# Two levels of Strassen for layer 1's scores, with part of the key sums added by transfers and the layer norm's root moved from k to q

## The chip, the core and the metric

The kernel runs on one core of one Trainium2 chip. The time is device microseconds of one execution; the figure for a kernel is the median of its runs. All data are fp32. The engines are named as the profile names them: PE is TensorE (PEld its weight loads), DVE is VectorE, ACT is ScalarE, POOL is GpSimd, SP is SyncE, which here only issues transfers.

## The reference

The input x is a batch of 8 items, each 512 channels by 1024 tokens (32 x 32). Two attention layers follow one another. Layer 0 is a layer norm over the channels and an attention of 8 heads of 64 channels; layer 1 is a group norm over 32 groups and an attention with a single head of 512 channels. Cut to what matters (biases and the affine parts of the norms left out):

```
# layer 0, per item
xn = layer_norm(x)                          # over channels
q, k, v = xn @ Wq.T, xn @ Wk.T, xn @ Wv.T   # 8 heads of 64
x = softmax(q k.T / 8) v @ Wo.T + x
# layer 1, per item
h = group_norm(x)                           # 32 groups
q, k, v = wq h, wk h, wv h                  # 512 x 1024 each
attn = softmax(q.T k * 512 ** -0.5)         # 1024 x 1024, over the keys
x = x + wp (attn v)
```

The change touches layer 1's scores `q.T k`, the sums of their exponentials over the keys, and the norm of layer 0 of a later item.

## The kernel before

**Products.** A product of two matrices, each cut into 2 x 2 blocks, is done by one level of Strassen (Winograd's form): seven block products in place of eight, with sums of blocks ahead of them (S1 to S4 of the left matrix, T1 to T4 of the right) and sums of results after them. The class `Product` runs the seven steps in the order of `STEPS`, each into a PSUM bank called x, y or z; some steps accumulate into a bank that already holds another product, so that most of the sums after are made by PE. `multiply()` issues a step's matmuls. `leave()` issues what follows it: after steps 1, 3 and 4 a copy of a bank by ACT (`u(0, 0)`, `u(0, 1)`, `u(1, 1)`), after steps 2, 5 and 6 an add of a bank to such a copy by DVE (an "out", L388), after step 7 a last copy. A unit is a `Product` for 128 rows of each block of the result. An out must read its bank before PE can open that bank again, one or two steps later.

**Two levels.** The projections of k and q of layer 0 (`project_deep`, matmuls at L591) already run two levels: six of the seven outer block products are again done by seven inner products, in three pairs ("tandems", two products at a time, so that each has the other's step in between), and one outer product (`22` by `T4`) whole (L634). Their operands come from `deep_operands_later`: four DVE instructions for a block, one of 512 columns and two or more of 256.

**Order.** Each engine works through its own instructions in the program's order. The order is written out by hand in one long loop over the items. `later(...)` puts closures into a list `side`; `tick(n)`, called in each step of a `Product`, takes `n` of them (the unit's `pieces`); `until(...)` takes them until a condition holds. So DVE's sums are strewn between PE's steps. A class `LayerNorm` makes the mean and the root for item b + 2 ahead of time, from its own list; `ln.waiting` holds its root back until the main loop sets it to False.

**An item's layer 1**, with the stages' names and their times in item 0: `qa` (280 to 307.7 us), the query in the basis of h, from the group norm's `gn` blocks; `s`, the scores, 28 steps (307.7 to 355.8); `vm`, the values (355.8 to 380.0); `o`, the output, whose moving operand is the exponentials p with the sums T1 to T4 of their blocks (380.0 to 428.0). Then k and q of the next item's layer 0 (428 to 467), and its attention.

**The scores** are one level in four units (`scores`, L500): each of the 28 steps has two matmuls of 512 columns. Exp is taken on 512 columns at a time after the outs (L1132), or straight out of PSUM. Key sums: p is [keys, queries], and the sum over keys is needed for each query. `key_sums` adds p's blocks on DVE (L1155, L1157) to two sums of 1024 elements per partition; POOL then issues transfers that add the upper half of a sum's partitions onto the lower (`halve`, L719) and lay the rest side by side (`fold`, L715). `inverse` transposes that on DVE (`fold1t`, L723), takes reciprocals, lets ACT copy the rows eight times (`rr`, L1200) and expands them (`rden`, L709), by which every out of `o` is multiplied (L1233).

**The next layer norm** runs in between: POOL adds x's blocks into `lns` by accumulating transfers and folds them (`fold_mu`); on DVE `foldm` (L723) is turned into means, ACT copies them (`lnmur`, L796), DVE expands them to `mu` and subtracts them from x (L816), ACT squares, DVE adds (`lnq`), POOL folds again, and the root (Ln and Exp on ACT, and eight small copies) is released in k's seventh step.

**Transfers.** SP's queue loads the weights (`load_w`), stores and loads the blocks put away (`x1_away`, `v_away`), loads x for item b + 2 and stores the output. POOL's queue has the accumulating transfers: those above, and those which add `x1_away` to an output block (L1235).

The functions that the change touches:

## Time and profile before

| | before |
|---|---|
| median of three runs | 2872.74 us (2872.62 to 2872.74) |
| the profiled execution's own time | 2871.5 us |
| its span | 2869.6 us |
| granted TensorE clock | 0.999 |
| PE busy | 2844.8 us, 10199 matmuls |
| DVE, ACT, POOL busy | 1818.1, 1168.0, 448.7 us |

An fp32 matmul of the program is two instructions in the profile. A PE row's duration includes the time in its pipeline and overlaps the next; what a matmul costs on a busy PE is the distance to the next start. A time on a row counts from the span's start. The window of item 2's layer 1 (`qa` from 984.8 us, scores from 1012.3, `vm` from 1060.3, `o` from 1084.5, k from 1132.6, q from 1155.9 to 1177.8) is taken where one item stands for the others, since items 0 and 7 have edges of their own.

### The profile page before, as it was taken

The numbers are of one execution on the slowest core, as the hardware profiler recorded it, in microseconds if no ns is written. First come the engines' busy times: TensorE is split into PE (matmuls) and PEld (weight loads), VectorE is DVE, ScalarE is ACT, GpSimd is POOL, SyncE is SP. The second block draws the span as 40 slices with busy tenths as digits, with TensorE's granted clock in tenths as the row PEclk, the third lists the DMA queues.
The fourth block names the chain that finished last, engine by engine and source line by source line (L and its number), as shares of the span: only waits on it lengthen the run. The fifth ranks groups of instructions, "written<-read, shape, count | busy, mean of one in ns | idle before, by whom it ended". The sixth has DMA issues, their size and how long they took to land.

```text
span 2869.6 us, 29155 instructions
## 1 busy us (share of the span) xinstructions
PE 2844.8 (99%) x10199; PEld 1482.1 (52%) x10199; DVE 1818.1 (63%) x2428; ACT 1168.0 (41%) x2015; POOL 448.7 (16%) x625
## 2 busy tenths in 40 slices
PE   9999999999999999999999999999999999999999
PEld 4535455354553555535555455544556445563345
DVE  6667367773667646776467754768456774457734
ACT  4462324723257132561336513365223733236331
POOL 2021021210212101120012200121011210112000
PEclk9999999999999999999999999999999999999999
DMA  8135246351563525434264342734326431262212
GB/s 314 50 73 141 72 98 184 71 154 63 131 155 70 148 72 162 116 77 140 88 180 86 84 135 81 198 77 114 118 74 184 108 104 59 73 170 63 88 37 67
DMA packets 124251, 321.33 MB, mean 112 GB/s; under 512 B 17872, under 2 KB 22272, under 8 KB 124096
## 3 DMA queue, kind: packets, MB, share of 16 engines
q0 software_dynamic: 45120, 110.66, 21.0%
q1 hardware_dynamic: 78880, 208.70, 20.6%
q8 instruction: 82, 1.34, 0.2%
q14 instruction: 73, 0.60, 0.1%
q10 hardware_dynamic: 96, 0.02, 0.0%
HBM read 187.72 MB, written 62.39 MB: 87 GB/s over the span
## 4 chain that ended last, share of the span: by engine, by line
PE 98%; DVE 1%; DMA 1%; ACT 0%; issue 0%; POOL 0%; SPq 0%; DVEq 0%; POOLq 0%
PE s L994 16%; PE acc L1012 15%; PE x_s L500 8%; PE x_o L508 8%; PE x_v L492 4%; PE x_qa L483 4%; PE x_vm L492 4%; PE y_o L508 4%; PE y_s L500 4%; PE x_out L483 4%; PE y_v L492 2%; PE y_vm L492 2%; PE y_out L483 2%; PE z_o L508 2%; PE z_s L500 2%; PE y_qa L483 2%
## 5 line engine op out<-in xcount | busy, mean ns | idle before, releaser
L1003 DVE TENSOR_TENSOR sum<-sum,p 128x1024 f32<-128x1024 f32 x384 | 470.3, 1225 | 38.7 <-DVE sum L1003 0.5
L997 ACT ACTIVATE p<-s 128x1024 f32<-128x1024 f32 (+1 forms) x608 | 478.8, 984 | 15.2 <-PE s L994 15.2
L994 PE MATMUL s<-q,k 64*128 64x512 f32 x2048 | 448.1, 592 | 0.0
L1012 PE MATMUL acc<-p,v_again 128*64 128x512 f32 x1792 | 390.9, 594 | 0.0
L994 PEld LDWEIGHTS s<-q,k 64*128 64x128 f32 x2048 | 195.9, 186 | 248.0 <-issue 152.9
L1012 PEld LDWEIGHTS acc<-p,v_again 128*64 128x64 f32 x1792 | 126.1, 137 | 261.3 <-issue 236.7
L715 POOL DMA_DIRECT2D fold<-sum x312 | 209.3, 762 | 311.1 <-DMA sum<-sum 191.7
L719 POOL DMA_DIRECT2D sum<-sum x78 | 63.5, 814 | 1109.8 <-DVE sum L1157 339.2
L1001 DVE TENSOR_TENSOR sum<-p,p 128x1024 f32<-128x1024 f32 x64 | 78.1, 1220 | 149.0 <-ACT p L997 149.0
L1016 ACT COPY o<-acc 128x512 f32<-128x512 f32 x63 | 36.9, 586 | 221.6 <-PE acc L1012 221.4
L500 PE MATMUL x_s<-S_qa,T_gn 128*128 128x512 f32 x256 | 120.3, 592 | 0.0
L508 PE MATMUL x_o<-T_p,S_vm 128*128 128x512 f32 x256 | 115.2, 592 | 0.0
L388 DVE TENSOR_TENSOR p<-u(1, 1)_s,x_s 128x512 f32<-128x512 f32 x32 | 22.0, 687 | 128.8 <-PE x_s L500 122.3
L492 PE MATMUL x_vm<-w_m,T_gn 128*128 128x256 f32 x384 | 90.7, 379 | 0.0
L483 PE MATMUL x_qa<-T_gn,w_a 128*128 128x512 f32 x192 | 89.4, 594 | 0.8 <-ACT qa L526 0.8
L483 PE MATMUL x_out<-T_o,w_o 128*128 128x512 f32 x192 | 89.2, 594 | 0.0
L513 ACT COPY u(0, 0)_v<-x_v 128x512 f32<-128x512 f32 x16 | 9.4, 586 | 187.5 <-PE x_v L492 187.5
L500 PEld LDWEIGHTS x_s<-S_qa,T_gn 128*128 128x128 f32 x256 | 48.6, 190 | 61.2 <-issue 61.2
L492 PE MATMUL x_v<-w_v,T_h 128*128 128x256 f32 x336 | 80.0, 381 | 0.0
L508 PEld LDWEIGHTS x_o<-T_p,S_vm 128*128 128x128 f32 x256 | 48.6, 190 | 60.7 <-issue 60.7
L1058 ACT COPY rr<-r 32x16 f32<-32x16 f32 x256 | 53.5, 209 | 62.4 <-DVE r L961 59.0
L1132 ACT ACTIVATE p<-p 128x512 f32<-128x512 f32 x96 | 60.2, 627 | 45.5 <-DVE p L388 45.5
(464 smaller groups left out, 4744.2 us busy)
## 6 DMA issues: line engine op xcount, KB each, us to landing
sum<-sum POOLq DMA_DIRECT2D x78, 256.0 KB, 3.4
fold<-sum POOLq DMA_DIRECT2D x312, 64.0 KB, 2.4
x<-in_x_dram SPq DMA_DIRECT2D x32, 512.0 KB, 6.0
xr<-in_x_dram SPq DMA_DIRECT2D x64, 256.0 KB, 2.8
x_away<-x SPq DMA_DIRECT2D x32, 512.0 KB, 2.6
v_away<-v SPq DMA_DIRECT2D x28, 512.0 KB, 3.0
v_again<-v_away SPq DMA_DIRECT2D x28, 512.0 KB, 8.3
w_o<-saved_o SPq DMA_DIRECT2D x24, 512.0 KB, 4.8
```

Of the source, the lines that this page charges most:

```text
L483: nc.tensor.matmul(dst, a[:, k, ts(r, P)], b[:, k, :], start=(opens and k == 0), stop=(k == 1), skip_group_check=True)
L492: nc.tensor.matmul(dst[:, ts(m, CB)], b[:, k, ts(2 * r + m, P)], a[:, k, :], start=(opens and m == 0 and k == 0), stop=(k == 1), skip_grou ...
L500: nc.tensor.matmul(dst, b[:, k, ts(r, P)], a[:, k, :], start=(opens and k == 0), stop=(k == 1), skip_group_check=True)
L508: nc.tensor.matmul(dst, a[:, m, ts(r, P)], b[m // 2][:, m % 2, :], start=(opens and m == 0), stop=(m == NM // 2 - 1), skip_group_check=True)
L715: nc.gpsimd.dma_start(out=f[ts(q + i, BL), :], in_=t[ts(n, BL), ts(i, HB)], accum_op=ALU.add if n else ALU.bypass)
L719: nc.gpsimd.dma_start(out=t[:D, :], in_=t[D:, :], accum_op=ALU.add)
L994: nc.tensor.matmul(parts[i], self.k[m // 4][r, ts(m % 4, P)], self.q[r, :], start=True, stop=True)
L997: nc.scalar.activation(dst, src, AF.Exp, scale=1.0 / float(D) ** 0.5)
L1001: nc.vector.tensor_add(self.sum, self.p[0], p)
L1003: nc.vector.tensor_add(self.sum, self.sum, p)
L1012: nc.tensor.matmul(acc[i * D : (i + 1) * D, :], value_of(self.vt, m, self.c * P + i * D, D), self.p[m][:, ts(i, HB)], start=(m == 0), stop ...
L1132: nc.scalar.activation(p, s, AF.Exp, scale=float(C) ** -0.5)
```

## The change

The scores are computed by two levels of Strassen. `SINGLES` lists the six outer products that are done by an inner level; they run in three pairs as the projections of k and q do, with matmuls of 256 columns, and the product `22` by `T4` is done whole, a quarter of it in each of four steps of the first two pairs. The sums of the outer level can no longer be left to PE, since each inner product ends in SBUF: DVE adds the seven results (`adds`, `add`), and Exp is taken when a block of p is complete, on 1024 columns. The operands for the inner level are made by DVE: `deep_query` for the query, `deep_operands_later` for gn. The residual adds (ACT, with the store of `x1_away`) move from the scores to `qa`.

Of the key sums, the first add of each of the two sums stays on DVE (`key_sum`); the four others become accumulating transfers of 512 KB on POOL's queue (`more_sums`), ahead of `halve` and `fold`. T1 of p is made at the end of the scores, T2 to T4 in `vm`. The load of w_m is issued after the first pair. In `o`, `inverse` is issued after two steps of both units instead of after the first step of the first, and the layer norm's list is queued after one more round of `side`. The root of the layer norm is released in q's third step instead of k's seventh.

Its core:

```diff
+SINGLES = [("11", "11"), ("12", "21"), ("S2", "T2"), ("S3", "T3"), ("S1", "T1"), ("S4", "22")]
...
+        def deep_query(self, *names):
+            def first(n):
+                x = self.q[n]
+                t = made[n] = big_tile(f"{n}_deep_qa_{self.b}").rearrange("p (i t) -> p i t", i=4)
+                nc.vector.tensor_add(t[:, 0], x[:, 0, CB:], x[:, 1, CB:])
+                nc.vector.tensor_sub(t[:, 2], x[:, 0, :CB], x[:, 0, CB:])
+            def rest(n):
+                x, t = self.q[n], made[n]
+                nc.vector.tensor_sub(t[:, 1], t[:, 0], x[:, 0, :CB])
+                nc.vector.tensor_sub(t[:, 3], x[:, 1, :CB], t[:, 1])
...
+            def plain(g, c):
...
+                ps = wides[(2 - g) % 3][:, ts(c, HB)]
+                for k in range(2):
+                    nc.tensor.matmul(ps, self.hb["T4"][:, k, ts(2 * g + c, P)], self.q["22"][:, k, :],
+                                     start=(k == 0), stop=(k == 1), skip_group_check=True)
+                return lambda: nc.scalar.copy(whole6[g][:, c, :], ps)
...
+            for j in range(3):
+                units = [unit(2 * j + n) for n in range(2)]
+                for i in range(len(STEPS)):
+                    for u in units:
+                        u.multiply()
+                    copy = plain(j, i - 3) if j < 2 and i in (3, 4) else nothing
+                    tick(self.pieces[j])
+                    for u in units:
+                        u.leave()
+                    copy()
+                m1, m2, m3, m5, m4, m7 = made
+                if j == 0:
+                    adds(m2, m1)
+                    finish("11", m2)
+                elif j == 1:
+                    self.key_sum(0, "11")
+                    adds(m3, m1)
+                    adds(m5, m3)
+                    adds(whole6, m5)
+                    finish("12", whole6)
                 else:
+                    adds(m3, m4)
+                    adds(m7, m3)
+                    self.key_sum(1, "12")
+                    later(lambda: add(m5[0], m4[0]))
+                    finish("21", m7)
+                    later(lambda: add(m5[1], m4[1]))
+                    later(lambda: self.more_sums(0, "21"))
+                    finish("22", m5)
+                    self.operands("T1")
+                    side.insert(len(side) - 1, lambda: (self.more_sums(1, "22"), self.fold()))
+                yield
...
+        def more_sums(self, i, n):
+            for t in self.p[n]:
+                nc.gpsimd.dma_start(out=self.total[i], in_=wide(t), accum_op=ALU.add)
...
-            wm_now = load_w("m", b)
...
+            for n, (_, name) in enumerate(SINGLES):
+                deep_operands_later(h1b, h1_deep, [name])
+                later(*(lambda ik=ik: residual(*ik) for ik in away[n : n + 1]))
...
+            steps = whole.scores(h1_deep)
+            next(steps)
+            wm_now = load_w("m", b)
+            next(steps)
+            next(steps)
+            whole.operands("T2", "T3", "T4")
...
-            o_units[0].step(1)
-            whole.inverse()
...
-            o_units[0].step(1)
+            o_units[0].step(2)
+            o_units[1].step(2)
+            whole.inverse()
...
-                    if n == 6 and ln:
-                        ln.waiting = False
...
+                    if n == 2 and ln:
+                        ln.waiting = False
```

More of the change, by code (lines that the diff above doesn't have):

```diff
@@ L553, in operand_inner, with deep_operands_later @@
                      lambda: all(x in deep for x in names))
-    def deep_operands_later(h, deep):
+    def deep_operands_later(h, deep, names):
         def first(n):
@@ L568, in deep_operands_later @@
         made = {}
-        for _, names in TANDEMS:
-            for n in names:
-                later(lambda n=n: first(n), lambda n=n: rest(n))
+        for n in names:
+            later(lambda n=n: first(n), lambda n=n: rest(n))
     def project_deep(tag, w, w_deep, bias, h, h_deep, pieces):
@@ L1108, in __init__ @@
             self.b, self.hb, self.x1 = b, hb, x1
+            self.q_deep = {}
+            self.pieces = (2, 2, 1)
             self.q = {f"{i + 1}{j + 1}": qa[j, i] for i in range(2) for j in range(2)}
@@ L1112, in __init__, with query_sum @@
             self.t = [{}, {}]
-        def query_sums(self):
-            for n in SUM_NAMES:
+        def query_sum(self, *names):
+            for n in names:
                 sum_later(self.q, n, lambda n: block(f"{n}_qa_{self.b}"), wide)
-        def scores(self):
-            b = self.b
-            shared = [{}, {}]
-            def unit(r):
-                g = r // 2
-                def dest(i, k):
-                    p = self.p[f"{k + 1}{i + 1}"]
-                    if p[g] is None:
-                        p[g] = block(f"p1_{b}_{k}{i}_{g}")
-                    return p[g][:, r % 2, :]
-                def exponential(p, s):
-                    nc.scalar.activation(p, s, AF.Exp, scale=float(C) ** -0.5)
-                def after(i, k):
-                    if (i, k) != (1, 0):
-                        exponential(dest(i, k), dest(i, k))
-                def shift(u, ps, which, add=None):
-                    if which == (1, 0):
-                        exponential(u, ps)
-                    else:
-                        nc.scalar.copy(u, ps)
-                return Product(f"s1_{b}_{r}", self.q, self.hb, key_part(r), shift, dest,
-                               banks_of(f"s1_{b}_{g}", r % 2, shared[g]), after)
-            return [unit(r) for r in range(4)]
@@ L1149, in key_sums @@
-        def key_sums(self, g):
-            def add(i, j):
-                p = wide(self.p[f"{j + 1}{i + 1}"][g])
-                if (g, j) == (0, 1):
-                    self.total[i] = big_tile(f"sum1_{self.b}_{i}")
-                    nc.vector.tensor_add(self.total[i], wide(self.p[f"1{i + 1}"][g]), p)
-                else:
-                    nc.vector.tensor_add(self.total[i], self.total[i], p)
-                self.summed = g == 1 and i == 1 and j == 1
-            for i in range(NH):
-                for j in range(1 - g, 2):
-                    later(lambda i=i, j=j: add(i, j))
@@ L1164, in operands @@
-        def operands(self, g):
-            def sub(n, l, r):
+        def deep_query(self, *names):
[8 more added lines that the diff above has]
+                nc.vector.tensor_sub(t[:, 3], x[:, 1, :CB], t[:, 1])
+                self.q_deep[n] = t
+            made = {}
+            for n in names:
+                later(lambda n=n: first(n), lambda n=n: rest(n))
@@ new lines, in exponential, with scores, part, query_inner @@
+        def exponential(self, t):
+            nc.scalar.activation(wide(t), wide(t), AF.Exp, scale=float(C) ** -0.5)
+        def scores(self, h_deep):
+            b = self.b
+            made = [[None, None] for _ in SINGLES]
+            whole6 = [None, None]
+            wides = [wide_psum(f"s1_{b}_{n}") for n in range(3)]
+            def part(dst, a, x, opens):
+                for c in range(2):
+                    nc.tensor.matmul(dst[:, ts(c, CB)], x[0][:, ts(c, P)], a[0], start=(opens and c == 0), stop=True,
+                                     skip_group_check=True)
+            def query_inner(n):
+                x = self.q[n]
+                blocks = [{f"{i + 1}{k + 1}": x[:, k, ts(i, CB)] for i in range(2) for k in range(2)}]
+                return Inner(blocks, lambda: [{s: self.q_deep[n][:, i] for i, s in enumerate(SUM_NAMES)}],
+                             lambda: n in self.q_deep)
+            def unit(m):
+                j, r = divmod(m, 2)
+                def dest(i, k):
+                    if made[m][k] is None:
+                        made[m][k] = block(f"p1_{b}_{m}_{k}")
+                    return made[m][k][:, :, ts(i, CB)]
+                def banks(to):
+                    if to == "y":
+                        return bank(f"y_s1_{b}_{m}")
+                    return wides[(r - j) % 3][:, :HB] if to == "x" else wides[(2 - j) % 3][:, ts(r, HB)]
+                a, x = SINGLES[m]
+                until(lambda: a in self.q and x in self.hb)
+                u = Product(f"s1_{b}_{m}", query_inner(a), operand_inner(self.hb, h_deep, [x]), part, plain_shift, dest,
+                            banks)
+                u.view = lambda t: t.rearrange("p (c t) -> p c t", c=2)
+                return u
+            def plain(g, c):
+                if c == 0:
+                    whole6[g] = block(f"p1_{b}_6_{g}")
+                    until(lambda: "22" in self.q and "T4" in self.hb)
+                ps = wides[(2 - g) % 3][:, ts(c, HB)]
[3 more added lines that the diff above has]
+                return lambda: nc.scalar.copy(whole6[g][:, c, :], ps)
+            def add(t, x):
+                nc.vector.tensor_add(wide(t), wide(t), wide(x))
+            def adds(ts_, xs):
+                later(*(lambda g=g: add(ts_[g], xs[g]) for g in range(2)))
+            def finish(n, t):
+                def exponentials():
+                    for g in range(2):
+                        self.exponential(t[g])
+                    self.p[n] = t
+                later(exponentials)
+            for j in range(3):
[18 more added lines that the diff above has]
+                    finish("12", whole6)
+                else:
+                    adds(m3, m4)
[9 more added lines that the diff above has]
+                yield
@@ new lines, in key_sum, with add, operands, sub @@
+        def key_sum(self, i, n):
+            def add():
+                until(lambda: self.p[n][0] is not None)
+                self.total[i] = big_tile(f"sum1_{self.b}_{i}")
+                nc.vector.tensor_add(self.total[i], *(wide(t) for t in self.p[n]))
+            later(add)
+        def more_sums(self, i, n):
+            for t in self.p[n]:
+                nc.gpsimd.dma_start(out=self.total[i], in_=wide(t), accum_op=ALU.add)
+        def operands(self, *names):
+            def sub(n, g):
+                l, r = {"T1": ("12", "11"), "T2": ("22", "T1"), "T3": ("22", "12"), "T4": ("21", "T2")}[n]
@@ L1170, in sub @@
                     self.p[n] = [self.t[0][n], t]
-            for n, l, r in (("T1", "12", "11"), ("T2", "22", "T1"), ("T3", "22", "12"), ("T4", "21", "T2")):
-                later(lambda n=n, l=l, r=r: sub(n, l, r))
+            for n in names:
+                later(*(lambda n=n, g=g: sub(n, g) for g in range(2)))
         def fold(self):
@@ L1460, in fast_path @@
                 ln.sums()
+            h1_deep = {}
+            away = list(x1)
+            for n, (_, name) in enumerate(SINGLES):
+                deep_operands_later(h1b, h1_deep, [name])
+                later(*(lambda ik=ik: residual(*ik) for ik in away[n : n + 1]))
             for u in a_units:
-                u.rest()
+                u.pieces = 2
+            a_units[0].rest()
             whole = Whole(b, qa, h1b, x1_away)
-            s_units = whole.scores()
-            whole.query_sums()
-            later(*(lambda ik=ik: residual(*ik) for ik in x1))
-            for u in s_units[:2]:
-                u.step(2)
-            for u in s_units[:2]:
-                u.rest()
-            whole.key_sums(0)
-            whole.operands(0)
-            for u in s_units[2:]:
-                u.rest()
-            whole.key_sums(1)
-            later(whole.fold)
-            whole.operands(1)
+            whole.deep_query("11")
+            a_units[1].step(5)
+            whole.deep_query("12")
+            whole.query_sum("S1", "S2")
+            whole.deep_query("S2")
+            whole.query_sum("S3")
+            whole.deep_query("S3")
+            whole.query_sum("S4")
+            whole.deep_query("S1", "S4")
+            steps = whole.scores(h1_deep)
[4 more added lines that the diff above has]
+            whole.operands("T2", "T3", "T4")
             v_units, vm = project_v(f"vm{b}", wm_now, h1b)
-            for u in v_units:
+            for u, n in zip(v_units, (4, 3)):
+                u.pieces = (2, 1)[v_units.index(u)]
+                u.step(n)
+                u.pieces = (1, 2)[v_units.index(u)]
                 u.rest()
@@ L1482, in fast_path @@
             check = iter(()) if more else all_checks()
-            o_units[0].step(1)
-            whole.inverse()
+            for u in o_units:
+                u.at_once = False
             if ln:
                 ln.xt = load_x(b + 2)
-            o_units[0].step(1)
+            o_units[0].step(2)
+            o_units[1].step(2)
+            whole.inverse()
+            for u in o_units:
+                u.at_once = True
+                u.finish()
             next(check, None)
-            o_units[1].step(2)
-            next(check, None)
+            tick(2)
             if ln:
+                later(nothing, nothing)
                 ln.queue()
@@ L1498, in fast_path @@
             o_units[0].rest()
+            next(check, None)
             o_units[1].step(1)
@@ L1501, in fast_path @@
                 h_deep = {}
-                deep_operands_later(hb, h_deep)
+                deep_operands_later(hb, h_deep, [n for _, names in TANDEMS for n in names])
             if b == 0:
```

## The prediction

> **What bounds the kernel now.** I read the page's parts 1 and 4 first, then PE's waits. PE is busy for nearly the whole span, and the chain of work that ended last lies on it:

> ```profile
> PE 2844.8 (99%) x10199; PEld 1482.1 (52%) x10199; DVE 1818.1 (63%) x2428; ACT 1168.0 (41%) x2015; POOL 448.7 (16%) x625
> PE 98%; DVE 1%; DMA 1%; ACT 0%; issue 0%; POOL 0%; SPq 0%; DVEq 0%; POOLq 0%
> ...
> PE z_k L591 <- ACT u(0, 1)_k L607: 5.9, 5, 1.2
> ```

> The last line is the largest of PE's waits (total us, times, longest): all of them together are below 20 us of 2869.6. So a change pays only by taking matmul time from PE, and costs only where it makes PE wait. The windows of item 0 (query projection, scores, values vm, output o) show how much room the helpers have beside PE; busy us and instruction count for each engine:

> ```profile
> 280.00:307.70 27.70, 27.70 (x74) 13.87 (x73) 12.64 (x18) 6.46 (x10) 2.93 (x5) 1.00 0.26 76
> 307.70:355.80 48.10, 48.10 (x114) 21.30 (x113) 19.93 (x23) 20.39 (x35) 0.00 (x0) 1.00 0.20 71
> 355.80:380.00 24.20, 24.20 (x114) 21.31 (x113) 12.45 (x14) 5.22 (x9) 6.87 (x10) 1.00 0.49 121
> 380.00:428.00 48.00, 48.00 (x113) 21.23 (x112) 36.39 (x58) 11.80 (x28) 9.46 (x12) 1.00 0.42 90
> ```

> DVE is half free up to the o stage and three quarters taken in it. PE's timeline of item 2 shows the rows that price the matmuls, a scores step, then the projection of k, which already runs two-level products in pairs, then that wait:

> ```profile
> 1012.26 1.88 PE L500 MATMUL x_s<-qa,gn 128*128 128x512 f32 x4
> 1013.98 1.88 PE L500 MATMUL z_s<-qa,gn 128*128 128x512 f32 x4
> ...
> 1132.57 0.59 PE L591 MATMUL x_k<-x,w_k 128*128 128x256 f32 x2
> 1133.00 0.59 PE L591 MATMUL x_k<-T_h,w_k 128*128 128x256 f32 x2
> 1133.43 1.03 PE L591 MATMUL x_k<-x,w_k 128*128 128x256 f32 x4
> 1134.29 0.59 PE L591 MATMUL z_k<-x,w_k 128*128 128x256 f32 x2
> ...
> 1152.36 1.13 PE L591 MATMUL z_k<-T_deep_h,w_k_deep 128*128 128x256 f32 x4 [1.18 <-ACT u(0, 1)_k L607]
> ```

> Starts, not ends, give the price: one scores step is 1.717 us (four instructions, two logical fp32 matmuls of 512 columns); a pair step of two products is 1133.43-1132.57 plus 1134.29-1133.43, 1.72 us for eight instructions of 256 columns, without a gap.

> [...] halving the columns costs little. Agrees: 0.429 us for 512 columns, 0.2159 for 256. [...] no added sum is cheap. Agrees: 1.22 us for 1024 elements (spaced 1.14), 0.68 for 512, 0.42 for 256. [...] below, the adds behind rden start only once rr is there. [...]

> ```profile
> sum<-sum POOLq DMA_DIRECT2D x78, 256.0 KB, 3.4
> fold<-sum POOLq DMA_DIRECT2D x312, 64.0 KB, 2.4
> lns<-in_x_dram POOLq DMA_DIRECT2D x24, 512.0 KB, 5.6
> k<-k POOLq DMA_DIRECT2D x14, 512.0 KB, 8.8
> q<-q POOLq DMA_DIRECT2D x14, 512.0 KB, 5.9
> ```

> **The change, part by part.** T is the start of the scores, all times per item, eight items.

> *Scores on PE.* Removed: 28 steps, 28 x 1.717 = 48.07 us. Added: three pairs of seven steps, 21 x 1.727 = 36.27, and the whole product with T4, eight matmuls of 512 columns, 8 x 0.858 = 6.87. 43.14 in all: 4.93 less an item, **39.5 us** less over eight. This is on the path.

> *DVE.* Added: six more outs (18 for 12) of 0.69, 4; deep query blocks, 6 x 4 x 0.42, 10; deep operands of gn, 6 x (0.68 + 2 x 0.42), 9; fourteen combining adds of 1.22, 17. Removed: four key-sum adds, 5. Some 35 us, which lifts DVE from 63% to about 73%. Where it falls: the gn operands and "11", "12" of the query beside the qa stage (15 us free), the rest beside the pairs (28 us free), the last adds and the T operands in vm. Placed by each step's due time, the first pair's outs come about 0.6 us before PE wants their bank, those of the later pairs 1 us or more. In vm about 21 of 24 us are taken; PE's slack at its fifth and sixth steps is 0.1 to 0.2. I charge 0.25 there, **+2** in all; from 0 to 1 us an item, since no row of before has vm so full. If the cover is gone, the outs of vm's steps five and six are late.

> *ACT.* Eight residual adds of 0.66 move into qa, where ACT has 21 us free; Exp runs in 1024-element pieces of about 1.05 in place of 0.63 halves. ACT is 40% busy in the old scores stage: nothing. From below, zero.

> *SP and POOL.* w_m's load moves behind the first pair on SP: landing took 8 to 9 us and 28 us remain, nothing. x1_away is stored earlier and the x loads of item b+2 wait for the end of the scores; w_k comes 17 to 20 us into vm and is wanted 50 us later. On POOL, four 512 KB accumulations (p onto the two sums) stand ahead of the halves and folds, and the output adds from x_away stand behind them; those had 20 us of POOL idle before.

> *The key sums' end.* From vm's start V: the first accumulation is issued at about V+7. Two serial chains share the queue, so it is one, then two together, then one. With 6.4 us for the first, 8.1 for the second of two at once (as k's and q's landed) and 6.5 for the last beside w_k, V+28; halve and folds took 10.8 us in before from the second halve's issue to the last fold: **F = V+39**. With 5.2 us each it is V+35, with the 8.8 us median V+45.

> *The inverse.* It moves behind steps 2 of both o units. In before, everything was early:

> ```profile
> 1086.46 0.70 DVE L723 STREAM_TRANSPOSE fold1t<-fold 128x512 f32<-128x512 f32 x1
> 1090.70 1.25 DVE L709 STREAM_TRANSPOSE rden<-rr 128x1024 f32<-128x1024 f32 x1 [1.56 <-ACT rr L1200]
> 1099.84 0.70 DVE L723 STREAM_TRANSPOSE foldm<-fold_mu 64x512 f32<-64x512 f32 x1
> 1103.21 1.25 DVE L709 STREAM_TRANSPOSE mu<-lnmur 128x1024 f32<-128x1024 f32 x1 [1.76 <-ACT lnmur L796]
> 1109.04 0.68 DVE L388 TENSOR_TENSOR u(1, 1)_o<-u(1, 1)_o,x_o 128x512 f32<-128x512 f32 x1
> ```

> o begins at 1084.5 here, so fold1t ran at o+2 and foldm 13 us later. Now DVE reaches fold1t at about o+14.6 (V+38.8), and foldm, mu and the centring stand right behind. From the start s of fold1t, by these durations: rr copied at s+4.2, rden to s+5.4, two multiplications, foldm at s+6.6, lnmur copied s+8.3 to s+10.0, and only then ACT's copy of u(1, 1)_o, done at s+10.6. PE wants that bank at o+24.0 (its fifth step; before, 1106.71 against 1108.53). So s may be o+13.4, and o+14.6 makes PE wait 1.2 us, the out of u(1, 1)_o another 0.2; F at V+39.5 rather than V+38.8 adds 0.7. 2.1 us for the six items with a layer norm to come: **+12.6**. The two others have until o+15.7: nothing. If F is earlier DVE's order still gives 1.4; if the mean's DVE work ran earlier, 0.

> *Root of the layer norm.* In k its eight small ACT copies (1.70 us) stand ahead of the copy that PE waits for at 1152.36; in q's step 2 they fall where no copy is due. **-5.9**. The scaling of x moves into q's last third, where DVE is the tighter engine: 0 to 1 us an item, I take **+1.5** in all.

> *Edges.* b = 0 also makes the deep weights on DVE: **+2**; b = 7 has leading layer-norm parts in place of cover: **+1.5**; both from 0 to 4.

> Sum: -39.5 - 5.9 + 2 + 12.6 + 1.5 + 3.5 = **-25.8**, on the profiled execution's own 2871.5 us (span 2869.6): 2845.7. The median of the runs is 1.2 above that time: **2847 us**.

> **The rivals.**
> *All hidden* (foldm early or F early, no vm wait): -39.5 - 5.9 with 3 for the edges, 2830 us. For it: k's pairs run gapless with DVE as full. Against: the order of DVE's program puts foldm behind fold1t. Chance 0.25.
> *DVE becomes the bound* inside the pairs and vm, outs some tenths late at several steps: 1.5 to 2.5 us an item on top of the forecast, 2860 to 2866. For it: slack 0.6 in the first pair. Against: the 28 us free there. Chance 0.17.
> *The key sums land late, slower than before.* fold1t waits in DVE's queue for the folds and holds rden, mu, centring and every out of o behind it; ACT's copies follow. Each us that F passes V+38.8 costs one in six items, past V+39.9 in all eight. The gain left, 39.5 + 5.9 - 7, is 4.8 us an item: from F near V+42.5 on it is gone. With 8.8 us at each step and the folds slowed too, F = V+45 to V+48: 6 to 9 us an item, 2880 to 2895. For it: k<-k's median. Against: that row falls where DMA is 84% busy; vm and o were at 42 to 49%. Chance 0.12. That the scores would not shrink is excluded by the count of instructions.

> **How the numbers follow.** Forecast case 0.46, 2840 to 2858. The range goes from 2829 (all hidden) to 2872 (part of the late case), leaving a tenth above and little below. 0.2% is 5.7 us, about what a measurement of this kernel can tell from no change: faster is below 2867, which takes the first three cases, less a little: 0.85; within 0.05; slower 0.10.

> **What would show it.** Right: scores stage 43 to 44 us of PE without gaps; no z_k wait on u(0, 1)_k; 1 to 3 us of PE waits at o's steps five and six on u(1, 1)_o; fold1t idle before it below 1 us. Wrong: PE waits on outs p in the pairs (DVE bound), or fold1t waiting many us for a fold (late sums), or o without waits (all hidden).

## The result, and the profile after

The changed kernel takes 2879.39 us (median of 18 runs, 2875.08 to 2885.55), the kernel before 2872.50 beside it (18 runs, 2871.54 to 2874.00). The ratio is 1.0026, interval 1.0019 to 1.0033: **slower by 0.26%**, where 0.9% faster was forecast. The profiled execution took 2883.7 us (span 2881.6), 4.3 above its median; the differences by stage below are from it, so they add up to 12 us and not to 7. The runs of the changed kernel also lie further apart than those of before, 10 us against 2.5.

The page's parts 1 and 4:

```profile
PE 2821.9 (98%) x10775; PEld 1593.4 (55%) x10775; DVE 2069.1 (72%) x2892; ACT 1233.6 (43%) x2079; POOL 477.1 (17%) x657
PE 82%; DMA 9%; DVE 4%; issue 2%; ACT 1%; POOL 1%; DVEq 0%; SPq 0%; POOLq 0%
```

and PE's waits (us in total, times, longest):

```profile
PE y_o L509 <- ACT u(1, 1)_o L514: 13.0, 6, 2.2
PE x_q L591 <- DVE q L389: 9.9, 5, 3.6
PE x_q L591 <- DVE w_q_deep L232: 9.8, 1, 9.8
PE x_o L509 <- ACT u(0, 1)_o L514: 5.2, 5, 1.2
```

PE has less to do, and still the end is later: 9% of the chain that ended last now lies on transfers and 4% on DVE, where each had 1%, and these four waits, of which only the third was there before (2.2 us), make 38 us. The windows of item 0 for scores, vm and o, with the columns of the prediction:

```profile
308.19:351.31 43.12, 43.12 (x185) 34.96 (x184) 32.50 (x51) 18.48 (x30) 0.00 (x0) 1.00 0.03 11
351.31:375.97 24.66, 24.44 (x113) 21.18 (x112) 20.80 (x21) 10.39 (x14) 4.04 (x5) 1.00 0.75 200
375.97:427.83 51.86, 48.84 (x114) 21.03 (x113) 37.52 (x60) 12.05 (x28) 12.40 (x17) 1.00 0.48 101
```

The scores shrink from 48.07 to 43.12 us without a gap; vm and o grow. From PE's starts of all stages, time after less time before, us:

| stage | forecast | measured | by item |
|---|---|---|---|
| scores (8 items) | -39.5 | -39.5 | -4.94 to -4.95 each |
| vm (8) | +2 | +3.9 | 0.48 to 0.49 each |
| o (items 0 to 6) | +12.6 | +27.5 | 3.8, 5.6, 5.6, 4.5, 4.1, 2.9, 1.0 |
| k (7) | -5.9 | -7.2 | -1.43 to -1.45 in five |
| q (7) | +3.5 | +27.4 | 8.3, 2.6, 3.2, 4.2, 3.6, 5.6, 0 |

In q's forecast stand the 1.5 for the scaling and the 2 for item 0; 1.5 was set down for item 7, of which the trace shows none. The scores came out right to a tenth of a microsecond, k gained 1.3 us more and vm lost 1.9 us more than forecast. What turned the result lies in o and q, 39 us above their forecasts, and the experiments are about these two.

**What o looks like.** PE's timeline in item 2 (o begins at 1090.37), from its seventh step on:

```profile
1112.38 3.70 PE L509 MATMUL x_o<-T_p,S_vm 128*128 128x512 f32 x8 [1.25 <-ACT u(0, 1)_o L514]
1118.25 5.40 PE L509 MATMUL y_o<-p,S_vm 128*128 128x512 f32 x8 [2.17 <-ACT u(1, 1)_o L514]
1123.48 1.02 PE L509 MATMUL x_o<-T_p,vm 128*128 128x512 f32 x2
```

and DVE's, the two transposes that begin the chains of the inverse and of the mean:

```profile
1107.50 0.71 DVE L723 STREAM_TRANSPOSE fold1t<-fold 128x512 f32<-128x512 f32 x1 [2.44 <-DMA fold<-sum]
1114.24 0.70 DVE L723 STREAM_TRANSPOSE foldm<-fold_mu 64x512 f32<-64x512 f32 x1
```

DVE is free for fold1t at o+14.7 (1107.50 less the 2.44 it waits), as forecast, but the last fold lands at o+17.1. Behind it the chain runs as worked out, foldm 6.7 us later. PE stands for it twice. And the step that begins at 1118.25 lasts until 1123.48, 5.23 us for eight instructions that take 8 x 0.429 = 3.43. The windows around it show why; the value after POOL's count is the granted clock:

```profile
1112.00:1118.00 6.00, 3.70 (x8) 1.44 (x8) 4.13 (x7) 2.33 (x10) 1.83 (x2) 1.00 0.39 58
1118.00:1119.00 1.00, 0.75 (x1) 0.39 (x2) 0.96 (x2) 0.20 (x1) 0.00 (x0) 0.70 0.95 164
1119.00:1121.00 2.00, 2.00 (x4) 0.81 (x3) 2.00 (x2) 0.85 (x1) 0.00 (x0) 0.50 0.55 194
1121.00:1122.00 1.00, 1.00 (x3) 0.43 (x2) 0.97 (x3) 0.92 (x2) 0.00 (x0) 0.59 0.92 260
```

After six us in which PE was busy for 3.70 the clock is halved, from 1118.41 to 1121.82 in the trace's clock record, 3.41 us, which costs 1.6 to 1.8 us more.

**What q looks like.** DVE's timeline in the q that follows item 2 (q begins at 1165.99):

```profile
1172.45 0.69 DVE L656 TENSOR_TENSOR k<-m_k,k 128x512 f32<-128x512 f32 x1 [3.59 <-DMA k<-k]
1174.38 1.28 DVE L389 TENSOR_TENSOR q<-u(0, 0)_q,z_q 128x512 f32<-128x512 f32 x2
1175.58 0.70 DVE L723 STREAM_TRANSPOSE foldv<-fold_var 64x512 f32<-64x512 f32 x1
1177.11 1.28 DVE L389 TENSOR_TENSOR q<-u(1, 1)_q,x_q 128x512 f32<-128x512 f32 x2
```

and PE's, which needs those last outs:

```profile
1177.84 0.70 PE L591 MATMUL x_q<-11_deep_h,w_q 128*128 128x256 f32 x2 [1.33 <-DVE q L389]
```

q's first outs come at q+8.4, against q+6.6 before, since DVE stands at L656 for an accumulation of k; then the root's foldv, its sum and scaling take 1.5 us more before the outs that PE waits for. In the kernel before (q begins at 1155.91), the root's scaling of x (L844) stood ahead of k's last sums, the accumulation had landed by the time DVE came to it, and nothing of the root stood between the outs:

```profile
1156.49 2.35 DVE L844 TENSOR_TENSOR x<-x,rstd 128x1024 f32<-128x1024 f32 x2
1159.96 1.28 DVE L656 TENSOR_TENSOR k<-m_k,k 128x512 f32<-128x512 f32 x2
1162.49 1.27 DVE L388 TENSOR_TENSOR q<-u(0, 0)_q,z_q 128x512 f32<-128x512 f32 x2
1163.95 0.69 DVE L388 TENSOR_TENSOR q<-u(1, 1)_q,x_q 128x512 f32<-128x512 f32 x1 [0.19 <-PE x_q L591]
```

### The profile page after: what moved, and what is told of

It reads as the page before. It is cut to its first block, busy times and chain, and to the rows that moved or that the text cites. A ratio compares the mean times of both kernels' runs of the same rounds, so it can differ in the third digit from the quotient of the medians.

```text
span 2881.6 us, 30944 instructions
## 1 busy us (share of the span) xinstructions
PE 2821.9 (98%) x10775; PEld 1593.4 (55%) x10775; DVE 2069.1 (72%) x2892; ACT 1233.6 (43%) x2079; POOL 477.1 (17%) x657
## 3 DMA queue, kind: packets, MB, share of 16 engines
q8 instruction: 87, 1.43, 0.2%
## 4 chain that ended last, share of the span: by engine, by line
PE 82%; DMA 9%; DVE 4%; issue 2%; ACT 1%; POOL 1%; DVEq 0%; SPq 0%; POOLq 0%
PE s L994 15%; PE acc L1012 15%; PE s L1151 7%; PE x_o L509 4%; PE x_v L493 4%; PE x_qa L484 4%; PE x_out L484 4%; PE y_o L509 3%; PE y_s L1151 3%; DMA sum<-p 3%; PE y_v L493 2%; PE y_out L484 2%; PE s L1186 2%; DMA fold<-sum 2%; PE y_qa L484 2%
## 5 line engine op out<-in xcount | busy, mean ns | idle before, releaser
L1246 POOL DMA_DIRECT2D sum<-p x32 | 28.4, 948 | 865.9 <-PE y_vm L493 672.9
L1191 DVE TENSOR_TENSOR p<-p,p 128x1024 f32<-128x1024 f32 x112 | 131.7, 1217 | 0.0
L493 PEld LDWEIGHTS x_vm<-w_m,T_gn 128*128 128x128 f32 x384 | 72.2, 190 | 14.6 <-DVE vm L389 4.9
L509 PE MATMUL y_o<-p,S_vm 128*128 128x512 f32 x128 | 63.3, 641 | 13.0 <-ACT u(1, 1)_o L514 13.0
## 6 DMA issues: line engine op xcount, KB each, us to landing
sum<-sum POOLq DMA_DIRECT2D x78, 256.0 KB, 3.4
x<-in_x_dram SPq DMA_DIRECT2D x32, 512.0 KB, 6.1
xr<-in_x_dram SPq DMA_DIRECT2D x64, 256.0 KB, 4.5
x_away<-x SPq DMA_DIRECT2D x32, 512.0 KB, 2.8
sum<-p POOLq DMA_DIRECT2D x32, 512.0 KB, 5.9
v_away<-v SPq DMA_DIRECT2D x28, 512.0 KB, 2.6
v_again<-v_away SPq DMA_DIRECT2D x28, 512.0 KB, 9.0
```

Source lines behind the costliest of these rows:

```text
L493: nc.tensor.matmul(dst[:, ts(m, CB)], b[:, k, ts(2 * r + m, P)], a[:, k, :], start=(opens and m == 0 and k == 0), stop=(k == 1), skip_grou ...
L509: nc.tensor.matmul(dst, a[:, m, ts(r, P)], b[m // 2][:, m % 2, :], start=(opens and m == 0), stop=(m == NM // 2 - 1), skip_group_check=True)
L1191: nc.vector.tensor_add(wide(t), wide(t), wide(x))
```

## The experiments

Theories on o: **C**, the key sums' transfers land late; **D**, the order on DVE and ACT alone. On q: **A**, POOL's queue (lnq's folds ahead of k's accumulations); **B**, the root's own work; **A'**, added after the first four, k's accumulations are slow beside bulk loads. A stage's loss below is always against the kernel before, summed over items 0 to 6, and comes from the one profiled execution of each version, which can lie some us off the median (f3's lies 4.8 us above it).

**e1, no transfers.**

```diff
         def more_sums(self, i, n):
-            for t in self.p[n]:
-                nc.gpsimd.dma_start(out=self.total[i], in_=wide(t), accum_op=ALU.add)
+            pass
```

> The changed kernel without its four accumulating transfers of p per item (the key sums are then those of four of the eight blocks; that part of the computation is left out). DVE's, ACT's and PE's orders are as in the changed kernel; only the folds land earlier. Theory C (late transfers make o wait): fold1t starts when DVE reaches it, about o+14.6, u(1, 1)_o costs PE 1.2 to 1.4 us in six items, the granted clock stays at 1.00 in o, o goes from +27.5 us over before (seven items) to about +9, the total from 2879 to about 2861. Rival D (the order on DVE and ACT alone makes o wait): o stays within 5 us of the changed kernel, total 2874 to 2880. q is not touched in either: its waits stay at 2 to 5 us an item and about 10 in item 0.

This version leaves four of the eight blocks of p out of the key sums. 2862.17 us, ratio 0.9961 (0.9947 to 0.9975). fold1t starts at o+14.61 in every item, without a wait; in the changed kernel its eight idle times sum to the following (view of the tile fold1t, us and times):

```profile
  DMA fold<-sum: 13.2, 7
```

o loses 1.65 us in each of six items, 9.9 instead of 27.5; its clock stays at 1.00. **C holds**: 17.6 us of o are the transfers' lateness with what follows from it, 9.9 are the order. q still loses 23.9.

**e2, lnq's folds first.**

```diff
-            yield from self.add("lnq", 1, self.sq[0, 1], self.sq[1, 1])
             if self.folded:
+                last = self.add("lnq", 1, self.sq[0, 1], self.sq[1, 1])
+                next(last)
+                yield
+                next(last)
                 self.fold("var")
```

> The changed kernel with the layer norm's second halve and folds (lnq, fold_var) issued right after the last lnq add, so on POOL ahead of the x_away adds of the second o unit instead of behind them. Nothing else moves. Theory A (POOL's queue: k's accumulations stand behind the late folds, DVE waits for k, q's outs come late): k<-k is issued at about k+17 as before, DVE's L656 waits less than 1 us, q's loss against before falls from 27.4 us (six items) to 3 to 6, the total to about 2857. Rival B (the root's own work in q makes q wait: foldv ahead of the outs, the small ACT copies, the scaling): q still loses 2 to 4 us an item, total 2873 or more. o stays as in the changed kernel.

2881.79 us, ratio 1.0039 (1.0026 to 1.0051). lnq's halve is issued in o and k<-k at k+17.2 as before the change (k+16.9). Item 0's q loses 2.5 us instead of 8.3, but items 1 to 5 still lose 21.5. **A is right for item 0 only.** In the others k<-k of 512 KB takes 9.7 us (median) and DVE waits as long as ever:

```profile
  DMA k<-k: 33.0, 13
```

**e3, the mean first.**

```diff
             o_units[0].step(2)
+            if ln:
+                ln.queue()
+                tick(1)
             o_units[1].step(2)
             whole.inverse()
...
-            if ln:
-                later(nothing, nothing)
-                ln.queue()
```

> The changed kernel with the layer norm's list queued after the first two o steps, ahead of the inverse, so foldm, lnmur, mu and the centring stand before fold1t on DVE and ACT; lnq and its folds come earlier with it. Theories A and C with the mean's part: PE's wait on u(1, 1)_o and the halved clock after it vanish (about 18 us), a wait on u(0, 1)_o of 1 to 2 us in five or six items stays since rr still waits for the late folds; q as in the run with the folds first (about 23 us less): total about 2838 to 2845. Rival B: q keeps its loss, total about 2860. Rival D, in the form that the mean ahead of the inverse only moves the wait to rden: o keeps 20 us or more.

2912.87 us, ratio 1.0141 (1.0124 to 1.0158): a miss. The wait on u(1, 1)_o is gone, but 45.3 us of waits on u(0, 1)_o come in its place, up to 8.1 each. mu's expansion and the centring still stood behind rden on DVE, and the squares of the centred x now stood ahead of the copy u(0, 1)_o on ACT. Only a part of the list had moved ahead of the late wait, and the rest of it did the harm. q loses 23.1.

**e4, sums on DVE.**

```diff
             for t in self.p[n]:
-                nc.gpsimd.dma_start(out=self.total[i], in_=wide(t), accum_op=ALU.add)
+                nc.vector.tensor_add(self.total[i], self.total[i], wide(t))
```

> The changed kernel with the four transfers replaced by four DVE adds of 1024 elements, in vm, as before the change. Theory C: the folds land early and o loses only what the order costs, about 9 us instead of 27; against that vm's DVE gets 4 x 1.14 = 4.6 us more where 21 of 24 us are taken, so PE waits 1 to 3 us for vm's outs or for the T operands at o's start, 8 to 24 us in all: total 2866 to 2885. Rival D: o keeps its 27 us and vm's loss comes on top, 2887 to 2903.

2869.12 us, ratio 0.9989 (0.9980 to 0.9998). o loses 9.9 again, as C says, and vm 1.3 us an item instead of 0.49, 9.1 for seven. So replacing these adds by transfers saved about 6 us in vm and cost 17.6 in o.

**f1 and f2, o's order back, and then the root in k.** On top of e4 and e2:

```diff
             o_units[0].step(2)
-            o_units[1].step(2)
             whole.inverse()
...
             next(check, None)
-            tick(2)
+            o_units[1].step(2)
             if ln:
-                later(nothing, nothing)
                 ln.queue()
```

f2 besides sets `ln.waiting` to False at k's `n == 6` again, not at q's `n == 2`.

> Key sums on DVE as in the run before it, and besides o's order nearly as before the change: the inverse after two steps of the first o unit, then the second unit's two steps, then the layer norm's list; lnq's folds right after its last add. The scores and the root in q stay. Theory A' (q waits because k's accumulating transfers land late among the bulk loads, which themselves come late because o ended late): loads and k<-k are back at their places against k's start, DVE's second L656 is done by k+28.5, q loses 1 to 2 us an item from foldv and the root's copies alone; o +0 to 3 us in all, vm +10, k -7: total about 2846 to 2850. Rival B (the root's own work in q): q still loses 2.6 to 4 us an item: 2852 to 2860.

> The run with o's order back, and the root of the layer norm released in k's seventh step, as before the change. Rival B: q's loss goes to below 0.5 us an item and k's wait on u(0, 1)_k of 1.2 us (1.45 with the restart) comes back: 7 us more in k, 13 or more us less in q. Theory A': q's loss was 1 to 2 us an item, so the two nearly cancel: within 3 us of the other kernel. Total about 2844 to 2850 in both; q against k tells.

f1: 2865.10 us, ratio 0.9977 (0.9968 to 0.9985). o loses 6.2 (1.04 an item, a wait of 0.7 on u(0, 1)_o behind the mean's small copies), q 20.9. A' had said that q would mend itself with o; it did not, and 2865 lies above what either theory gave. f2: 2850.90 us, ratio 0.9927 (0.9910 to 0.9943). q loses 1.2, and k's gain is lost (+0.8 instead of -7.2). In f2 k's accumulation is late too, but only 1.72 us of that are idle, since the root's work fills the time ahead, and q's outs follow one another (DVE's timeline):

```profile
1155.09 0.69 DVE L656 TENSOR_TENSOR k<-m_k,k 128x512 f32<-128x512 f32 x1 [1.72 <-DMA k<-k]
1157.02 1.28 DVE L389 TENSOR_TENSOR q<-u(0, 0)_q,z_q 128x512 f32<-128x512 f32 x2
1158.22 1.28 DVE L389 TENSOR_TENSOR q<-u(1, 1)_q,x_q 128x512 f32<-128x512 f32 x2
```

(q begins at 1148.63: first outs at q+8.4, as in the changed kernel, the second ones at q+9.6 instead of q+11.1.) So B holds in part: with these late accumulations the root's work in q is what makes PE wait in this item.

**f3 and f4, v_again late.** f3 on top of e2, f4 on top of f1:

```diff
+                    if n == 6:
+                        vts = {ik: big_tile(f"v{b + 1}_again_{ik[0]}{ik[1]}") for ik in vn_away}
+                        for ik, d in vn_away.items():
+                            nc.scalar.dma_start(out=vts[ik], in_=d)
                 qt["last"]()
-                vts = {ik: big_tile(f"v{b + 1}_again_{ik[0]}{ik[1]}") for ik in vn_away}
-                for ik, d in vn_away.items():
-                    nc.sync.dma_start(out=vts[ik], in_=d)
```

> The changed kernel with lnq's folds first, and the four 512 KB loads v_again issued from ACT's queue in q's seventh step instead of from SP ahead of it; so 2 MB less move while k's accumulating transfers do. Transfers of the key sums and o's order stay as in the changed kernel, so o keeps its 27 us. Theory A': k<-k of 512 KB lands in 5 to 7 us instead of 9.7 and 12.8, DVE's waits in L656 fall from 6.4 us to below 1.5, q's loss from 24 us to 8 or less: total about 2864 to 2868. Rival B: q's loss stays above 18: 2876 or more. If v_again comes too late, PE waits at the first acc of layer 0 instead.

> The run with o's order back and, besides, v_again issued late from ACT's queue. Theory A': q's loss goes to about 1 us an item, total about 2840. Rival B: as the run with o's order back, within 2 us.

f3: 2863.31 us, ratio 0.9966 (0.9953 to 0.9978), with o still losing 29.5. k<-k takes 5.6 us, and DVE's waits for it (view of line L656) are, in the changed kernel and then in f3:

```profile
  DMA k<-k: 36.1, 14
```

```profile
  DMA k<-k: 1.4, 4
```

q loses 8.3, of which 5.5 are a new wait on ACT, which now issues the loads. **A' holds as well**: with the root in q and the accumulations on time there is no such stall. f4: 2850.60 us, ratio 0.9926 (0.9910 to 0.9943). q loses 6.8, about the 1 us an item that A' gave, but the total is ten us above the 2840 that A' gave: o keeps the 6.2 us of f1's order.

**h1, the root in k alone**: the changed kernel with e2's edit and the root at k's seventh step; all transfers as they were.

> The changed kernel with lnq's folds first and the root back in k's seventh step; transfers of all four adds, o's order and v_again stay as in the changed kernel. If the root's DVE work and the late k accumulations stall q only together: q's loss falls from 24 us to below 4, k gives back 7, o keeps 27: total about 2863 to 2869. If the late accumulations alone stall q: q keeps 10 us or more, 2873 and up.

2866.63 us, ratio 0.9981 (0.9973 to 0.9989). q loses 1.6, k 1.6, o 30.3, though k<-k still takes 9.5 us (median). With f3 this says that late accumulations and the root in q stall q only together: taking away either removes most of the loss (h1 keeps 1.6 us, f3 2.8 beside its wait on ACT).

**g1, g2, g3, put together.** On top of e2's edit and f1's order, with the list for the mean two rounds later (`later(nothing, nothing)`), so that its copies stand behind u(0, 1)_o. g1: the first sum's adds by transfers, the second's on DVE, and v_again as in f3 but from POOL's queue in q's fifth step. g2: as g1, v_again from SP, root in k. g3: as g1, all key sums on DVE.

> A version put together from the causes: the two adds of the first key sum stay transfers (ready first), the two of the second are DVE adds; inverse after two steps of the first o unit; the layer norm's list queued two rounds later than in the run with o's order back, so that the small copies for mu stand behind ACT's copy u(0, 1)_o; lnq's folds first; root in q; v_again issued from POOL's queue behind k's second accumulations. Expected if the causes found so far (late folds, DVE full in vm, the mean's copies ahead of u(0, 1)_o, v_again beside k's accumulations) are all: vm +0.5 to 1 us an item, o below 0.5, k -1.44, q below 0.5: total about 2833 to 2839. If k's accumulations stay late, or POOL's issue of v_again holds q's accumulations: q 2 us an item more, 2845 to 2850.

> As the version with v_again on POOL, but v_again from SP as in the changed kernel and the root of the layer norm in k's seventh step as before the change. k's wait on u(0, 1)_k comes back (7 us in five items), q loses below 0.5 us an item: total about 2840 to 2845. If the root in q were no cost by itself, this would be the slower of the two by just those 7 us.

> As the version with v_again on POOL, but all key sums on DVE: the difference is what the two transfers save in vm. vm +1.3 us an item instead of 0.5 to 1: 2 to 6 us slower than that version, 2837 to 2843. If transfers are no help at all (they land late and o waits for them), this is the faster one.

| | median us | ratio (interval) | vm | o | k | q |
|---|---|---|---|---|---|---|
| g1 | 2839.30 | 0.9885 (0.9868 to 0.9901) | +3.4 | +6.2 | -7.0 | +3.5 |
| g2 | 2852.41 | 0.9931 (0.9914 to 0.9948) | +3.7 | +8.9 | +2.9 | +4.1 |
| g3 | 2838.77 | 0.9884 (0.9867 to 0.9900) | +9.1 | 0.0 | -7.2 | +3.1 |

g3 is the fastest here, 1.2% below the kernel before, though not measurably better than g1. Expected for it was 2 to 6 us more than for g1: two transfers keep vm short, but their folds still arrive 2.6 to 4.1 us after DVE is ready in six items, and o takes back what vm gained. g2 missed its 2840 to 2845: PE waits for other copies of ACT in k as well, in four items, and o and q lose more than in g1. v_again's queue differs between g1 and g2 too, so the 13 us between them are not the price of the root's place alone. PE's waits in g3 (largest first): nothing in o is left.

```profile
PE x_vm L493 <- DVE vm L389: 8.3, 8, 1.0
PE pst_q L304 <- DMA w_q<-in_L_conv_wq_dram: 5.0, 2, 4.5
PE x_q L591 <- DVE w_q_deep L232: 2.2, 1, 2.2
```

## Why the prediction was wrong, step by step

*Scores on PE.* Right: 43.12 us against 43.14, no gaps, no rival needed. Halving the columns cost as little as the prediction took it to: eight instructions of 256 columns take 1.727 us and four of 512 take 1.717, which is 2.5 ns more for a pair of 256 than for one of 512.

*DVE in vm.* Mis-sized by 0.24 us an item: 0.25 forecast, 0.49 measured, of which the wait itself is 0.22 and the rest the restart: the step behind the wait takes 1.83 us instead of 1.73, and its start comes about 0.16 later than the wait accounts for.

*The inverse.* The place was right (DVE ready at o+14.6, PE's limit about o+13.4), and so was the order's own cost: 1.4 forecast, 1.65 measured (e1). **The term that failed is F with its price.** F was summed to V+38.8 and charged as V+39.5, 0.7 us of lateness for six items; fold1t waited 1.1 to 2.4 us in these (it started at o+15.8 to o+17.1, V+40.5 to V+41.8), and 1.9 us in item 6, for which nothing was set down and where o loses 1.0. In item 2, each step counted until the next one that waits for it, the first accumulation, issued on time (V+7.2), took 7.5 us instead of 6.4; of the two together the later one was issued 2 us behind the other, and the last followed 10.1 us after the first of them instead of 8.1; the last took 5.3 instead of 6.5, halve and folds 11.7 instead of 10.8. I had set the slow row k<-k aside because DMA was only 49% busy in vm, but that share is from the kernel before, without the change's own transfers: in the window of vm shown above it is 75%. What of this load slowed the accumulations, no run separates. From issue to landing they took 4.5 to 10.0 us, 5.9 in the median.

And I priced a wait at its own length. In items 1 to 3 the halved clock added about 1.6 us each, 4.8 in all. Which stall loses the clock does not follow its length alone: item 3 with 2.2 us of waits did, item 4 with 3.4 did not. Nor does it follow the item: in the trace of h1 item 4 shows the long step behind its waits (5.24 us for eight instructions, after 3.1 us of waits) and item 3 does not (3.66, after 2.4). What decides it, these runs do not isolate (last section).

*Root of the layer norm.* k's gain came, 7.2 for 5.9, as each wait removed also saves a restart of 0.27: a wait of 1.18 us had put k's end off by 1.45. **The failed step is the +1.5 for q.** I looked at ACT's eight copies and at the scaling, and not at what the root puts on DVE between q's first and second outs (foldv, sum and scaling, 1.5 us), nor at the accumulations of k that DVE waits for just ahead. Before, that wait was already there, 4.8 us in five of its places with 8.8 us per transfer, and the root's work in k filled the rest. I had quoted that very row, k<-k 8.8, for another purpose. The k stall hid something too: without it q begins 1.44 us earlier against the same transfers. In item 2 the second accumulation landed at k+28.2, before at k+27.3, so 1.4 of the 2.4 us that it is later against q are k's own gain. f2 and h1 give k its time back along with the root; that the root's work decides is seen apart from this only where f2 has its first outs at the same q+8.4. And q lost the clock as well: in items 3 and 5 it was halved once, and PE is busy for 23.9 us there against 22.7 in items 1, 2 and 4.

*Edges.* Item 0 was put at +2 and lost 8.3 in q (which ends at 478.4 us in the kernel before, not at 467). The prediction did not ask what stands behind lnq's halve and folds on POOL once these come later: k's accumulations, issued 5 us later in item 0, and behind them on DVE the deep weights of q (the wait of 9.8). e2 gives that back.

*The rivals.* The late key sums were the right mechanism for 17.6 us, but at V+40.5 to V+41.8 they alone would have left the kernel faster, as the prediction's deciding point of V+42.5 has it (h1: 2866.6 with o losing 30). It took q's 27 us beside it to turn the sign; no rival had that. DVE as the bound inside the pairs did not happen. Three sums do not come out as written, and the forecast case rests on none of them: with 5.2 us each F is V+33.4, not V+35; 9 us an item for the late sums gives about 2906, not 2895; and DVE has 23 us free beside the pairs, not 28, since the stage itself shrinks by 5.

## What to carry to other kernels

Where a wait has been removed from one place, ask what the wait was covering: here the root's work in k filled the time until late transfers had landed. A step moved to a later place brings its instructions in front of whatever stood there, on each of its queues; for each, name the next instruction that the bottleneck waits for and its slack. And on a PE that is 99% busy, price a stall of one or two microseconds with a possible halved clock on top (about 1.6 us in each of three items here), not at its length alone. A share of DMA read before a change does not hold the change's own transfers (vm: 49% before, 75% after).

## What the runs showed of the hardware that was not expected

```profile
1115.00:1118.41 3.41, 1.24 (x4) 0.35 (x3) 1.61 (x3) 2.21 (x9) 0.84 (x1) 1.00 0.77 117
1118.41:1121.82 3.41, 3.41 (x5) 1.33 (x6) 3.38 (x4) 1.59 (x2) 0.00 (x0) 0.50 0.72 208
1821.55:1824.96 3.41, 1.65 (x4) 0.87 (x5) 2.24 (x2) 1.63 (x7) 0.00 (x0) 1.00 0.93 189
1824.96:1828.37 3.41, 3.41 (x9) 1.25 (x8) 3.38 (x5) 2.11 (x2) 0.22 (x1) 1.00 0.71 216
```

PE was busy for 1.24 us of the one step, and the next had half the clock; it was busy for 1.65 us of the other, and the clock stayed. No run varies the place or the length of such a gap by itself, so this is told of these two items and not as a rule.

Four loads issued from ACT's queue held ACT's next copy back (0.33 and 1.42 us of issue in f3), and PE lost 0.8 us at it in each item; with the same loads on POOL's queue (g3) PE waits for no copy of ACT in q. A 512 KB accumulation took 9.7 us beside 2 MB of plain loads (e2) and 5.6 us with these moved away (f3; medians of 14).
